# Planner costs, a merged activation block and per-block B tiles on GpSimd in a two-layer state-space kernel

## The chip, the cores and the metric

The kernel runs on one core of a Trainium2 chip. The core has a matrix engine (PE, with its weight loads shown as PEld), a vector engine (DVE), an activation engine (ACT), GpSimd (POOL) and a sync engine (SP) that issues DMAs. Each engine works through its own queue of instructions in order, and semaphores tie the queues together. The metric is the device time of one execution in microseconds, as the median of several runs.

## What is computed

Two layers on x of shape 8 x 48 x 48 x 192, all in float32. Each layer normalises its input by groups, applies a selective state-space block and adds the result to its input. The heart of both is a scan over tokens, with 384 channels and 16 states a channel. Layer 0 runs it in four directions over the image (rows, columns, both reversed):

```
xi, z = split(in_proj(x)); z = silu(z); xi = silu(conv3x3(xi))
for each of 4 directions:
    dts, B, C = x_proj(xs);  dt = softplus(dt_w @ dts + bias)
    h = exp(dt * A) * h + (dt * u) * B        # state by state, along the tokens
    y = sum over states of h * C              # + D * u
y = layernorm(y0 + y1 + y2 + y3) * z;  out = out_proj(y)
```

Layer 1 runs the same kind of scan along columns and then along rows, each forward and backward, with a causal convolution of three taps along the line:

```
xs, z = split(in_proj(x)); u = silu(conv(xs) + cb)
dt, B, C = split(x_proj(u)); dt = softplus(dt_proj(dt) + dtb)
h = h * exp(dt * A) + (dt * u) * B;  y = sum over states of h * C + u * D
y = y * silu(z);  out = out_proj(y)     # forward and backward are added
```

## The kernel before

**Tiling.** Channels lie on the 128 partitions in three groups (NJ = 3); tokens are cut into chunks of 384 (T). One chunk in one direction is an item. Each layer has 192 items. In layer 1 two items, forward and backward of the same chunk, make a pair, and there are 96 pairs: 48 for the columns and 48 for the rows. An item consists of 48 segments: 16 states by three channel groups. A due time in the code is counted in segments, so a pair spans 96.

**What a segment needs.** ACT makes the decay exp(dt * A) for one state and channel group (L423). The other factor of the scan, dt * u * B, is built with tokens on partitions, because there B of one state is one number for each partition. The product dt * u is made by POOL (du, L363), turned by PE and copied out as dtu. For each state a tile bT of three 128 x 384 blocks holds dtu times B. Either ACT makes it in three instructions with a scale for each partition (L452), or POOL makes it in one multiply of 128 x 1152 with B as a broadcast operand (L447). PE turns the blocks back into PSUM (b, L471), three transposes for a segment, and DVE runs the scan (L987 in layer 0, L1224 in layer 1). After three scans POOL multiplies all of h by C (L506), and PE adds it up over the states by transposing it into y (L523). One of the 16 states goes another way: B itself is turned, and DVE multiplies it by du (L482).

**Around the scans.** For each pair, project (L294 to L349) computes dt, B and C on PE (xd_ps, bt_ps, dt_ps), evicts them from PSUM on ACT or DVE, sends B and C to DRAM to be spread again by SP (cc), and ends with softplus on dt. In layer 1, inputs makes the convolution's input (xi_ps, L1114; taps on ACT and DVE, L1133 and L1139), gates makes z (z_ps, L1164), and begins applies silu to u of a pair and to z of the pair before it in one block on ACT (L1207) and then calls project. The function leave copies y out and turns it back; finish multiplies by z (L1228); output projects it (o_ps, L1256). Softplus and silu need another activation table than exp does: each block loads its table or tables, and then the one of exp again (L212).

**The order.** All of it is emitted by hand in an order that a planner (class Plan) makes while the program is built. Each piece of work is a Need: a due time, a cost for each engine that may take it, and the marks that it waits for. The planner keeps a clock for each engine. At each step it takes the engine that could start earliest, and gives it the ready Need with the earliest due time, within a margin NEAR. A mark counts for another engine only LAG later. So the costs in the code do two things: they choose between ACT, DVE and POOL where a Need has several, and they set in which order each engine's queue is written. COPY and BIAS are the costs of evictions, TABLE that of a table load, MM that of one pass of a wide matrix product. The function pace spreads the due times of a series of Needs over a range lo to hi.

**Depths.** Decays have 12 buffers in layer 0 and 16 in layer 1. The tiles bT have three and four; PSUM tiles b three; h four; in layer 1, u five and z four; input tiles xt three.

Of the kernel before, what the change touches and what calls it, by code (L numbers as in the profile page):

```python
# [11 lines left out]
F32 = mybir.dt.float32  # L12
# [28 lines left out]
LAG = {PE: 0.3, DVE: 0.2, ACT: 0.2, POOL: 0.2, SP: 0.0}  # L41
DMA = 3.5
NEAR = 0.2
TABLE = 1.29
COPY = {ACT: 0.41, DVE: 0.5}
BIAS = {ACT: 0.51, DVE: 0.6}
# [134 lines left out]
class Common:  # L181
# [97 lines left out]
    def project(self, plan, pool, p, pair, lo, mid, hi):  # L279

        nc, mark = self.nc, plan.mark
        tiles = {}
        dts, evacs = [], []
        for i, item in enumerate(pair):
# [34 lines left out]
            n = Need(at(), {ACT: 0.3, DVE: 0.35}, after, frees=k, sets=[mark("bt", g)])  # L321
# [5 lines left out]
            for j in range(NJ):  # L327
                after = [got]
                if j == 0 and g >= 3:
                    after.append(mark("exp", (g - 2) * NSEG - 1))  # L330
                n = Need(at(), {PE: 0.55}, after, bank=True)
                yield n
                ps = self.bank(n, "dt_ps")
                if j == 0:
                    dt = pool.tile([P, NJ, T], F32, tag="dt", name="dt", bufs=3)
                    dts.append(dt)
                nc.tensor.matmul(  # L337
                    ps[:, :T], wts["dtw"][:, j * P : (j + 1) * P], xd[:R, :], start=True, stop=True
                )
                evacs.append(plan.then(  # L340
                    Need(at(), BIAS, [n], frees=n.bank),
                    lambda e, dt=dt, j=j, ps=ps, wts=wts: self.biased(
                        e, dt[:, j, :], ps[:, :T], wts["dtb"][:, j : j + 1]
                    ),
                ))
            self.xd_used = [n, sent]
        yield Need(hi, {ACT: 2 * 1.16 + 2 * TABLE}, evacs, sets=[mark("dt", 2 * p), mark("dt", 2 * p + 1)])
        for item, dt in zip(pair, dts):
            nc.scalar.activation(dt, dt, AF.Softplus)  # L349
            item["dt"] = dt  # L350
        self.tables()
# [38 lines left out]
    def stream(self, plan, pool, items, direct, decay, scan, finish, held, kept, weighed):  # L390
# [34 lines left out]
        def weighs():  # L425
            past = []
            for i, item in enumerate(items):
                for n in states:
                    b = 0
                    while b < TB:  # L430
                        after = [mark("dtu", i, b), mark("bt", i)]
                        costs = {ACT: 0.51}
                        if b == 0:
                            if len(past) >= weighed:
                                after += [mark("place", past[-weighed] + j) for j in range(NJ)]
                            after += [mark("dtu", i, c) for c in range(1, TB)]
                            costs[POOL] = 2.2
                        need = Need(
                            i * NSEG + NJ * n - 5 + b * 0.5, costs, after, sets=[mark("bT", i, n, b)],
                            late={ACT: LATE},  # L440
                        )
                        yield need
                        if b == 0:
                            to = bts[i, n] = pool.tile([P, TB, DI], F32, tag="bT", name="bT", bufs=weighed)
                        of, by = item["dtu"], item["bt"][:, :, R + n : R + n + 1]
                        if need.e == POOL:
                            nc.gpsimd.tensor_tensor(to, of, by.to_broadcast((P, TB, DI)), ALU.mult)  # L447
                            for b in range(1, TB):
                                m = mark("bT", i, n, b)
                                m.t, m.e = need.t, need.e  # L450
                        else:
                            nc.scalar.activation(to[:, b, :], of[:, b, :], AF.Copy, scale=by[:, b, :])  # L452
                        b += 1
                    past.append(i * NSEG + NJ * n)
# [18 lines left out]
        def scans():  # L473
            for s in range(total):
# [3 lines left out]
                if n in direct:  # L478
                    done = [mark("multiplied", i)] if n == max(direct) and j == NJ - 1 else ()
                    yield Need(s, {DVE: 0.55}, [mark("place", s), mark("du", i)], sets=done)  # L480
                    b = bps[s][:, :T]
                    nc.vector.tensor_tensor(b, b, item["du"][:, j, :], ALU.mult)  # L482
# [11 lines left out]
        def gathers():  # L494

            for f in range(total // NJ):
# [3 lines left out]
                if "carry" in item:  # L500
                    yield Need(NJ * f + 2.5, {POOL: 0.19}, after, sets=[mark("carry", i, n)])
                    item["carry"](n, hs[f])
                yield Need(NJ * f + 3, {POOL: 2.64}, after + [mark("cc", i, n // 2)], sets=[mark("gather", f)])
# [75 lines left out]
def layer0(ctx, cm, x, xs, x2, w, norm):  # L579
# [43 lines left out]
    def matrices(j, due, after):  # L623

        diag = None
        for t in range(9):
            n = Need(due, {POOL: 0.4}, after)
            yield n
            if t == 0:
                diag = pool.tile([P, 9, P], F32, tag="diag", name="diag", bufs=1)  # L630
            nc.gpsimd.tensor_tensor(
                diag[:, t, :], cm.ident, cw[:, j, t : t + 1].to_broadcast((P, P)), ALU.mult
            )
# [95 lines left out]
    def convolved(diag, of, c, after, at):  # L729
        for t in range(9):  # L730
            n = Need(at(), {PE: 0.49}, after if t == 0 else (), bank=(t == 0))
# [101 lines left out]
    def enters():  # L833

        for p in range(len(items) // 2):
# [3 lines left out]
            if q < 3:  # L839
# [8 lines left out]
                yield Need(lo, {ACT: 2.13 + 2 * TABLE}, after, sets=[mark("u", b, q)])  # L848
# [3 lines left out]
            yield from cm.project(plan, pool, p, items[g : g + 2], lo, mid, hi)  # L852

    def tails():
# [4 lines left out]
        for b in range(NIMG):  # L859
            st = None  # L860
            for c in range(NC - 1, -1, -1):
# [13 lines left out]
                n = Need(at(), {DVE: 1.45}, [n], frees=k)  # L875
# [4 lines left out]
                n = Need(at(), {ACT: 1.16}, [n] + used)  # L880
# [16 lines left out]
                n = Need(at(), {DVE: 1.77}, [n])  # L897
# [13 lines left out]
                n = Need(at(), {ACT: 1.16 + 2 * TABLE}, [got_z])  # L911
# [4 lines left out]
                for j in range(NJ):  # L916
                    n = Need(at(), {POOL: 1.0}, [n])
# [47 lines left out]
    for b in range(NIMG):  # L965
        for k in range(4):
            rev = k >= 2
            order = range(NC - 1, -1, -1) if rev else range(NC)
            for n, c in enumerate(order):
# [5 lines left out]
                    cost=(0.75, 3.1, 0.96) if k % 2 else (0.65, 2.64, 0.96),  # L975
# [16 lines left out]
    def finish(i, item, j, need, y):  # L992
        b, k, c = item["b"], item["k"], item["c"]

        def add(e):
# [9 lines left out]
            Need(need.due + 1, {DVE: 0.85 if k % 2 else 0.6}, [need], frees=need.bank,  # L1005
# [12 lines left out]
def layer1(ctx, cm, x2, xw, dst, w, norm):  # L1018
# [53 lines left out]
    def inputs():  # L1072

        last = []
        for p in range(pairs):
            stage, b, c = place_of(p)
            lo, hi = 2 * p * NSEG - 176, 2 * p * NSEG - 96
# [15 lines left out]
            if stage == 0:  # L1093
                n = Need(at(), {ACT: 1.02}, [n])
# [32 lines left out]
    def taps(i, j, u, ps, k, n, at):  # L1127
# [3 lines left out]
        n = Need(plan.at + 1, {ACT: 0.51}, [n])  # L1131
# [4 lines left out]
        n = Need(plan.at + 1, {DVE: 2 * 0.59}, [n], frees=k, sets=[mark("tapped", i, j)])  # L1136
# [7 lines left out]
    def gates():  # L1144

        last = []
        for p in range(pairs):
            stage = place_of(p)[0]
            lo, hi = 2 * p * NSEG - 76, 2 * p * NSEG + 2
# [5 lines left out]
            for d in range(2):  # L1155
                for j in range(NJ):
                    for m in range(NM):
                        after = [mark("x", p), wz[d][1]] + ([mark("out", p - 2)] if p > 1 else [])
# [9 lines left out]
                    if j == 0:  # L1168
                        z = items[2 * p + d]["z"] = pool.tile([P, NJ, T], F32, tag="z", name="z", bufs=4)
# [6 lines left out]
    def begins():  # L1176

        last, block = [], [mark("never")]
        diag = None
        for p in range(pairs + 1):  # L1180
            stage = place_of(p)[0]
            s = 2 * p * NSEG
            if p % per == 0 and p < pairs:
                xp, n0 = yield from part("xp", w["xp"][:, 2 * stage : 2 * stage + 2], s - 100, cm.xd_used)
                dtw, n1 = yield from part("dtw", w["dtw"][:, 2 * stage : 2 * stage + 2], s - 100, cm.xd_used)
                n = Need(s - 90, {DVE: 1.5})
# [5 lines left out]
            after = []  # L1192
            for d in range(2):
                if p < pairs:
                    after += [mark("tapped", 2 * p + d, j) for j in range(NJ)]
                if p > 0:
                    after += [mark("gate", 2 * p - 2 + d, j) for j in range(NJ)]
            if 0 < p < pairs:
                after.append(mark("exp", s - 96 + 18))
            count = 2 * (p > 0) + 2 * (p < pairs)  # L1200
            done = [mark("silu", 2 * p - 2)] if p > 0 else ()
            n = Need(s - 87, {ACT: 2 * TABLE + 1.16 * count}, after, sets=done)
            yield n
            for d in range(2):
                for i, name in ((2 * p + d, "own"), (2 * p - 2 + d, "z")):
                    if 0 <= i < len(items) and (name == "z") == (i < 2 * p):
                        nc.scalar.activation(items[i][name], items[i][name], AF.Silu)  # L1207
            cm.tables()
            if p == pairs:
                return  # L1210
            for d in range(2):
                items[2 * p + d].update(
                    diag=diag[:, d], A=A[:, 2 * stage + d], ready=[n] + loaded,
                    wts=dict(xp=xp[:, d], dtw=dtw[:, d], dtb=dtb[:, 2 * stage + d]),
                )
            yield from cm.project(plan, pool, p, items[2 * p : 2 * p + 2], s - 84, s - 52, s - 30)
# [9 lines left out]
    def finish(i, item, j, need, y):  # L1226
# [3 lines left out]
        plan.then(Need(need.due + 1, {DVE: 0.55}, [need], frees=need.bank, sets=[mark("gated", i, j)]), gate)  # L1230
# [3 lines left out]
    def output(p):  # L1234
# [13 lines left out]
        for m in range(NM):  # L1248
# [12 lines left out]
            n = Need(at(), {DVE: 0.6}, [n] + (got if stage else before), frees=k)  # L1261
# [14 lines left out]
        dict(cost=(0.65, 2.64, 0.9), wanted=lambda j, i=i: [mark("silu", i - i % 2)]) for i in range(2 * pairs)  # L1276
# [81 lines left out]
```

## Time and profile before

| | us |
|---|---|
| median of 3 runs | 21915.49 (21907.13 to 21929.59) |
| profiled execution, its own time | 21913.88 |
| span in the profile | 21912.2 |
| first scan of layer 1 | 11120 after the start |

The costliest groups of instructions, with the mean duration of one:

| engine and line | what | count | busy us | mean ns |
|---|---|---|---|---|
| POOL L506 | h times C, 128 x 1152 | 6144 | 16183.7 | 2647 |
| DVE L1224 | scan, layer 1 | 9216 | 8149.8 | 936 |
| PE L471 | B tiles turned into PSUM | 51840 | 8090.6 | 277 |
| ACT L452 | B tile, one block | 13998 | 8067.2 | 608 |
| PE L523 | sum over states | 55296 | 7944.2 | 276 |
| ACT L423 | decays, both layers | 18432 | 10338.2 | 602 to 608 |
| POOL L363 | du | 384 | 1075.2 | 2800 |
| ACT | table loads, all lines | 755 | 968.7 | 1283 |

Durations overlap: the next instruction of an engine often starts before the one before it has ended. On ACT, six decays in a row take 3.09 us together, so they start 0.50 us apart, while each lasts 0.60. A busy engine is therefore not necessarily one at its limit, and distances between starts say more about what it can do than durations do. DMA moves 69 GB/s on average, with the 16 engines at about a fifth of their time. The TensorE clock granted is 0.992.

### The profile page before, as it was taken

How to read it: one execution, taken by the hardware profiler on the slowest of the kernel's cores; microseconds unless marked ns; L12 is line 12 of the kernel's file. 1: busy time of each engine (PE TensorE's matmuls, PEld its weight loads, DVE VectorE, ACT ScalarE, POOL GpSimd, SP SyncE). 2: the span in 40 equal slices, each digit the busy share in tenths (PEclk: the TensorE clock that was granted, in tenths of full speed). 3: DMA queues.
4: the chain of work that ended last, by engine and by line, in shares of the span. 5: the costliest groups of instructions: out<-in, count | busy, mean ns of one | idle time of the engine just before them, and what ended most of it. 6: DMA issues, size and time to landing. Idle time of an engine off the chain costs nothing.

```text
span 21912.2 us, 391042 instructions
## 1 busy us (share of the span) xinstructions
PE 20543.4 (94%) x138640; PEld 15779.7 (72%) x138640; DVE 19575.8 (89%) x24030; ACT 20649.0 (94%) x38918; POOL 20082.0 (92%) x10562
## 2 busy tenths in 40 slices
PE   9989899899998999988889999999999999999999
PEld 6767667676676766766667777777777777777777
DVE  7998898989889898899978888888888999999998
ACT  7999999999999999999989999999999999999999
POOL 7999999999999999999979999999999999999999
PEclk9999999999999999999999999999999999999999
DMA  2222222222222222221222221211122222222222
GB/s 76 75 83 68 75 78 74 83 68 74 77 74 83 68 75 76 74 74 61 66 61 63 62 63 62 63 62 62 62 64 65 66 66 66 66 65 66 66 66 64
DMA packets 728901, 1512.31 MB, mean 69 GB/s; under 512 B 181508, under 2 KB 324484, under 8 KB 726824
## 3 DMA queue, kind: packets, MB, share of 16 engines
q1 hardware_dynamic: 724768, 1485.21, 21.7%
q8 instruction: 1105, 18.10, 0.3%
q14 instruction: 844, 6.91, 0.1%
q10 hardware_dynamic: 2184, 2.08, 0.0%
HBM read 1382.03 MB, written 104.99 MB: 68 GB/s over the span
## 4 chain that ended last, share of the span: by engine, by line
PE 55%; ACT 21%; POOL 11%; DVE 7%; issue 5%; DMA 1%; POOLq 0%; DVEq 0%; SPq 0%; ACTq 0%
PE y L523 16%; PE b L471 16%; POOL h L506 9%; ACT bT L452 8%; ACT l_da L423 5%; PE xd_ps L294 4%; ACT a L423 4%; PE dt_ps L337 4%; PE cv_ps L735 4%; DVE h L1224 3%; PE o_ps L1256 3%; PE z_ps L1164 2%; DVE h L987 2%; PE xi_ps L1114 2%; PE xi_ps L684 1%
## 5 line engine op out<-in xcount | busy, mean ns | idle before, releaser
L506 POOL TENSOR_TENSOR h<-h,cc 128x1152 f32<-128x1152 f32 x6144 | 16183.7, 2647 | 988.3 <-DVE h L1224 346.8
L1224 DVE TENSOR_TENSOR_SCAN h<-l_da,b 128x384 f32<-128x384 f32 x9216 | 8149.8, 936 | 709.6 <-PE b L471 541.8
L471 PE MATMUL b<-ident,bT 128*128 128x128 f32 x51840 | 8090.6, 277 | 471.2 <-DVE h L987 311.9
L523 PE MATMUL y<-ident,h 128*128 128x128 f32 x55296 | 7944.2, 276 | 621.2 <-POOL h L506 588.2
L452 ACT ACTIVATE bT<-dtu,bt 128x384 f32<-128x384 f32 x13998 | 8067.2, 608 | 77.9 <-PE b L471 67.9
L523 PEld LDWEIGHTS y<-ident,h 128*128 128x128 f32 x55296 | 6310.9, 141 | 2189.2 <-POOL h L506 1176.6
L471 PEld LDWEIGHTS b<-ident,bT 128*128 128x128 f32 x51840 | 6061.7, 141 | 2411.4 <-issue 971.6
L987 DVE TENSOR_TENSOR_SCAN h<-a,carry,b 128x384 f32<-128x384 f32 x7680 | 7223.1, 995 | 636.3 <-PE b L471 299.0
L423 ACT ACTIVATE a<-dt,l_A 128x384 f32<-128x384 f32 x9216 | 5220.6, 608 | 27.5 <-DVE h L987 25.4
L423 ACT ACTIVATE l_da<-dt,l_A 128x376 f32<-128x376 f32 x9216 | 5117.6, 602 | 77.6 <-DVE h L1224 75.5
L447 POOL TENSOR_TENSOR bT<-dtu,bt 128x1152 f32<-128x1152 f32 x1094 | 2324.2, 2125 | 200.8 <-PE b L471 174.9
L987 DVE TENSOR_TENSOR_SCAN h<-a,b 128x384 f32<-128x384 f32 x1536 | 1359.9, 936 | 166.5 <-PE b L471 114.4
L294 PE MATMUL xd_ps<-u,l_xp 128*44 128x384 f32 x2304 | 1128.8, 586 | 3.9 <-ACT u L1133 2.7
L363 POOL TENSOR_TENSOR du<-dt,u 128x1152 f32<-128x1152 f32 x384 | 1075.2, 2800 | 62.3 <-ACT dt L349 61.6
L337 PE MATMUL dt_ps<-xd,l_dtw 12*128 12x384 f32 x2304 | 1043.5, 534 | 10.4 <-ACT z L220 8.0
L1114 PE MATMUL xi_ps<-xt,l_u 96*128 96x384 f32 x2304 | 936.3, 490 | 12.7 <-ACT xt L1097 6.3
L735 PE MATMUL cv_ps<-pad,diag 128*128 128x384 f32 x2376 | 939.2, 490 | 0.5 <-ACT v L227 0.3
L1256 PE MATMUL o_ps<-z,l_out 128*96 128x384 f32 x2304 | 931.7, 489 | 0.9 <-ACT dt L227 0.8
L962 POOL COPY carry<-h 128x3 f32<-128x3 f32 x2560 | 504.4, 197 | 442.1 <-DVE h L987 303.4
L1164 PE MATMUL z_ps<-xt,l_z 96*128 96x384 f32 x2304 | 885.3, 489 | 1.1 <-ACT xd L220 0.6
L227 ACT ACTIVATE dt<-dt_ps,l_dtb 128x384 f32<-128x384 f32 x931 | 539.8, 580 | 292.5 <-PE dt_ps L337 283.8
L1139 DVE SCALAR_TENSOR_TENSOR u<-xi_ps,l_conv_w,u 128x376 f32<-128x376 f32 (+1 forms) x1152 | 686.6, 596 | 65.4 <-ACT u L1133 43.4
(122 smaller groups left out, 14499.2 us busy)
## 6 DMA issues: line engine op xcount, KB each, us to landing
cc<-bc SPq DMA_DIRECT2D x3072, 384.0 KB, 3.5
xc<-in_x SPq DMA_DIRECT2D x186, 288.0 KB, 4.4
z<-v SPq DMA_DIRECT2D x144, 192.0 KB, 1.9
z<-z SPq DMA_DIRECT2D x48, 576.0 KB, 4.3
v<-v SPq DMA_DIRECT2D x126, 192.0 KB, 1.8
u<-v SPq DMA_DIRECT2D x21, 1152.0 KB, 8.3
xc<-in_xs SPq DMA_DIRECT2D x48, 288.0 KB, 3.6
x<-xc SPq DMA_DIRECT2D x48, 288.0 KB, 3.0
```

Of the source, the lines that this page charges most:

```text
L294: nc.tensor.matmul(rows(ps[:E, :T]), wts["xp"][:, j, :], item["u"](j), start=(j == 0), stop=(j == NJ - 1),)
L337: nc.tensor.matmul(ps[:, :T], wts["dtw"][:, j * P : (j + 1) * P], xd[:R, :], start=True, stop=True)
L423: nc.scalar.activation(dst, src, AF.Exp, scale=item["A"][:, j, n : n + 1])
L447: nc.gpsimd.tensor_tensor(to, of, by.to_broadcast((P, TB, DI)), ALU.mult)
L452: nc.scalar.activation(to[:, b, :], of[:, b, :], AF.Copy, scale=by[:, b, :])
L471: nc.tensor.transpose(ps[:, b * P : (b + 1) * P], of, self.ident)
L506: nc.gpsimd.tensor_tensor(h, h, c, ALU.mult)
L523: nc.tensor.matmul(item["sum"][b][:, j * P : (j + 1) * P], hs[f][:, j, b * P : (b + 1) * P], self.ident, is_transpose=True, skip_group_che ...
L735: nc.tensor.matmul(rows(ps[:, :T]), diag[:, t, :], of[:, c * RT + t // 3 : (c + 1) * RT + t // 3, t % 3 : t % 3 + S], start=(t == 0), stop ...
L987: nc.vector.tensor_tensor_scan(order(h[:, at % NJ, :]), order(a), order(b[:, :T]), carry[:, at : at + 1] if item["carried"] else 0.0, ALU. ...
L1224: nc.vector.tensor_tensor_scan(h[:, at % NJ, :], a, b[:, :T], 0.0, ALU.mult, ALU.add)
L1256: nc.tensor.matmul(ps[:CP, :T], wout[:, 2 * stage + e, j, m * CP : (m + 1) * CP], items[2 * p + e]["z"][:, j, :], start=(e == 0 and j == 0 ...
```

## The change

Four things change.

1. The numbers that the planner reckons with are replaced nearly everywhere: lags, the margin, costs of copies, bias evictions, scans, projections and so on.
2. In weighs, each 128 x 384 block of bT is now a Need of its own that ACT or POOL may take. POOL does one block by a tensor_scalar instruction whose scalar is a column of B, in place of one tensor_tensor over the whole tile.
3. project no longer ends with softplus. In layer 0, enters does it at the same place. In layer 1 a new function block puts softplus of a pair, silu of that pair's z and silu of the next pair's u behind one another on ACT, with a table load for softplus, one for silu and one back to exp at the end. Only the first pair's are still done in parts.
4. In layer 1, the due times of inputs, gates and project lie earlier; z has six buffers in place of four, and a pair's z waits for the output of three pairs before in place of two.

```diff
-LAG = {PE: 0.3, DVE: 0.2, ACT: 0.2, POOL: 0.2, SP: 0.0}
+LAG = {PE: 0.2, DVE: 0.14, ACT: 0.15, POOL: 0.1, SP: 0.0}
-NEAR = 0.2
+NEAR = 0.1
-COPY = {ACT: 0.41, DVE: 0.5}
-BIAS = {ACT: 0.51, DVE: 0.6}
+COPY = {ACT: 0.37, DVE: 0.47}
+BIAS = {ACT: 0.48, DVE: 0.53}
...
-                n = Need(at(), {PE: 0.55}, after, bank=True)
+                n = Need(at(), {PE: 0.83}, after, bank=True)
...
-        yield Need(hi, {ACT: 2 * 1.16 + 2 * TABLE}, evacs, sets=[mark("dt", 2 * p), mark("dt", 2 * p + 1)])
         for item, dt in zip(pair, dts):
-            nc.scalar.activation(dt, dt, AF.Softplus)
             item["dt"] = dt
-        self.tables()
+        return evacs
...
-                        costs = {ACT: 0.51}
-                        if b == 0:
-                            if len(past) >= weighed:
-                                after += [mark("place", past[-weighed] + j) for j in range(NJ)]
-                            after += [mark("dtu", i, c) for c in range(1, TB)]
-                            costs[POOL] = 2.2
+                        if b == 0 and len(past) >= weighed:
+                            after += [mark("place", past[-weighed] + j) for j in range(NJ)]
                         need = Need(
-                            i * NSEG + NJ * n - 5 + b * 0.5, costs, after, sets=[mark("bT", i, n, b)],
-                            late={ACT: LATE},
+                            i * NSEG + NJ * n - 5 + b * 0.5, {ACT: 0.51, POOL: 0.6}, after,
+                            sets=[mark("bT", i, n, b)], late={ACT: LATE},
                         )
...
-                            nc.gpsimd.tensor_tensor(to, of, by.to_broadcast((P, TB, DI)), ALU.mult)
+                            nc.gpsimd.tensor_scalar(to[:, b, :], of, by, None, ALU.mult)
...
-                    cost=(0.75, 3.1, 0.96) if k % 2 else (0.65, 2.64, 0.96),
+                    cost=(1.29, 3.1, 0.915) if k % 2 else (0.7, 2.6, 0.915),
...
-            lo, hi = 2 * p * NSEG - 176, 2 * p * NSEG - 96
+            lo, hi = 2 * p * NSEG - 230, 2 * p * NSEG - 146
...
-            lo, hi = 2 * p * NSEG - 76, 2 * p * NSEG + 2
+            lo, hi = 2 * p * NSEG - 130, 2 * p * NSEG - 50
...
-            yield from cm.project(plan, pool, p, items[2 * p : 2 * p + 2], s - 84, s - 52, s - 30)
+            after = yield from cm.project(plan, pool, p, items[2 * p : 2 * p + 2], s - 120, s - 80, s - 46)
+            if p == 0:
+                yield from block(s - 44, here, [], [], after)
+                yield from block(s - 10, [], here, there)
+            else:
+                yield from block(s - 44, here, here, there, after + [mark("exp", s - 36)])
+
+    def block(due, dts, zs, us, after=()):
+
+        after = list(after) + [mark("gate", i, j) for i in zs for j in range(NJ)]
+        after += [mark("tapped", i, j) for i in us for j in range(NJ)]
+        sets = [mark("dt", i) for i in dts] + [mark("silu z", i) for i in zs] + [mark("silu", i) for i in us]
+        tables = 1 + bool(dts) + bool(zs or us)
+        yield Need(due, {ACT: tables * TABLE + 1.07 * len(dts + zs + us)}, after, sets=sets)
+        cm.softplus([items[i] for i in dts])
+        for i in zs:
+            nc.scalar.activation(items[i]["z"], items[i]["z"], AF.Silu)
+        for i in us:
+            nc.scalar.activation(items[i]["own"], items[i]["own"], AF.Silu)
+        cm.tables()
...
-        dict(cost=(0.65, 2.64, 0.9), wanted=lambda j, i=i: [mark("silu", i - i % 2)]) for i in range(2 * pairs)
+        dict(cost=(0.71, 2.6, 0.855), wanted=lambda j, i=i: [mark("silu z", i)]) for i in range(2 * pairs)
```

## The prediction

> **What bounds the kernel now.** I read the page's first part, then busy time in stretches, then the timeline of one stretch. The first part names no single bound:
>
> ```profile
> PE 20543.4 (94%) x138640; PEld 15779.7 (72%) x138640; DVE 19575.8 (89%) x24030; ACT 20649.0 (94%) x38918; POOL 20082.0 (92%) x10562
> ```
>
> Four engines are nearly full, so what matters is whether they are full at the same moments. Layer 0 ends with its last scan at 11007 us; layer 1 begins scanning at 11120 and repeats every 112.2 us, once per pair of items (96 pairs). One such pair, cut in four, columns being the stretch, its length, then busy time and instructions by engine:
>
> ```profile
> 14962.00:14990.00 28.00, 26.52 (x193) 20.95 (x192) 23.46 (x30) 27.94 (x49) 27.85 (x12) 1.00 0.20 59
> 14990.00:15018.00 28.00, 28.00 (x177) 20.76 (x177) 25.65 (x36) 24.61 (x49) 24.65 (x10) 1.00 0.24 70
> 15018.00:15046.00 28.00, 28.00 (x186) 20.91 (x185) 24.66 (x31) 25.58 (x49) 23.39 (x10) 1.00 0.24 65
> 15046.00:15075.00 29.00, 27.86 (x212) 23.85 (x211) 27.84 (x38) 28.80 (x56) 28.39 (x12) 1.00 0.17 56
> ```
>
> In the middle half PE (first column) never rests, and ACT and POOL (fourth and fifth) lose 3.4 + 2.4 and 3.4 + 4.6 us. In the outer half ACT and POOL are full and PE is not. The bound alternates. The timeline of ACT, DVE and POOL shows what the middle looks like:
>
> ```profile
> 15018.53 1.63 ACT L452 ACTIVATE bT<-dtu,bt 128x384 f32<-128x384 f32 x3 [1.72 <-PE b L471]
> 15024.30 0.95 DVE L1224 TENSOR_TENSOR_SCAN h<-l_da,b 128x384 f32<-128x384 f32 x1 [1.15 <-PE b L471]
> 15019.79 2.63 POOL L506 TENSOR_TENSOR h<-h,cc 128x1152 f32<-128x1152 f32 x1 [3.33 <-issue]
> ```
>
> Everyone waits for PE's transposes (L471), which stand in PE's queue behind projections (o_ps, dt_ps, xi_ps, z_ps, xd_ps all fall there); POOL's row names no releaser, but what it multiplies are the scans that come late. At the start of each pair it is ACT that holds things up, with a block of silus between two table loads; a scan waits for the exponential behind it:
>
> ```profile
> 15089.31 1.28 ACT L1207 ACT_TABLE_LOAD   x1
> 15090.60 1.17 ACT L1207 ACTIVATE u<-u 128x1152 f32<-128x1152 f32 x1
> ...
> 15094.95 1.28 ACT L212 ACT_TABLE_LOAD   x1
> 15096.24 5.11 ACT L423 ACTIVATE l_da<-dt,l_A 128x376 f32<-128x376 f32 x10
> 15096.88 1.80 DVE L1224 TENSOR_TENSOR_SCAN h<-l_da,b 128x384 f32<-128x384 f32 x2 [0.92 <-ACT l_da L423]
> ```
>
> **What each engine must do.** For every form I take its step, the lower quartile of the time from its start to the next start on its engine; this leaves waits out. Steps times counts over 60 steady pairs give, per pair of 112.2 us: ACT 105.1, PE 103.4, POOL 102.7, DVE 99.4. (PE: 612 transposes by 0.109, 36 diagonal products by 0.111, 72 wide passes by 0.322, 12 of dt_ps by 0.412, 12 of xd_ps by 0.357, 6 small.) The rest is loss: ACT 7.1, PE 8.8, POOL 9.5, DVE 12.8. In layer 0, over 300 to 11000 us, the same sums are POOL 93.6%, ACT 93.0%, DVE 88%, PE 81%.
>
> **The change, part by part.** Counts are from the two programs' instruction orders.
>
> Merged block, layer 1: table loads fall from 382 to 285, so ACT saves 97 x 1.295 = 126 us. The activations in it are the same.
>
> New planner costs: in layer 1 ACT hands DVE 105 bias evictions, 80 xd, 113 yt, 65 z and 84 small copies. ACT saves 50 + 30 + 41 + 23 + 13 us (steps 0.479, 0.376, 0.36, 0.36, 0.15). DVE pays about 56 + 38 + 51 + 30 + 14 us, with some dtu copies 199: 2.1 us a pair. In layer 0 it is 124 bias evictions and 32 of v, ACT about -68, DVE about +82 us, which its 12% of slack there hides.
>
> B tiles: ACT makes 242 blocks less in layer 0 and 97 less in layer 1 (0.506 each: -122 and -49 us). POOL goes from 419 whole tiles to 1501 blocks, and from 675 to 2120. Its old tile has a step of 2.058 us in layer 0 and 2.072 in layer 1. The new operation is nowhere in the trace, so I bound it. Rows on POOL:
>
> ```profile
> L447 POOL TENSOR_TENSOR bT<-dtu,bt 128x1152 f32<-128x1152 f32 x1094 | 2324.2, 2125 | 200.8 <-PE b L471 174.9
> L631 POOL TENSOR_TENSOR diag<-ident,l_conv_w 128x128 f32<-128x128 f32 x207 | 79.8, 417 | 90.8 <-PE cv_ps L735 90.8
> L919 POOL TENSOR_TENSOR acc<-acc,z 128x384 f32<-128x384 f32 x144 | 142.6, 1005 | 22.5 <-ACT z L913 22.5
> L777 POOL MEMSET acc<- 128x5000 f32 x1 | 4.3, 4264 | 0.0
> ```
>
> Upper end: a multiply with a broadcast operand has steps 0.358 at 128 elements and 2.072 at 1152, hence 1.674 ns an element and 0.144 us fixed; at 384, 0.787 us. Lower end: the two memsets (2181 ns at 2500, 4264 at 5000) give 0.83 ns and 0.10 us, at 384 0.42 us. In between: two full streams cost 2.14 ns an element (steps 0.954 at 384, 2.60 at 1152), a step-zero second one 1.67; dropping it saves as much again, 1.20 ns, so 0.46 + 0.144 = 0.60 us. I take 0.60, since the broadcast multiply, from which this is drawn down, is the nearest kin. POOL then changes by 901 - 862 = +39 us in layer 0 and 1272 - 1399 = -127 in layer 1.
>
> The Trainium skill (GPSIMD Engine Reference, 4.1 Engine selection) calls one-input work on this engine roughly line-rate; at the 1.2 GHz of its Specifications that is, as an estimate, 0.32 us plus dispatch for 384 elements, and with the trace's 0.10 us fixed POOL would fall by some 230 us in layer 0 and 510 in layer 1. Against the change speaks its section 2.1 Instruction dispatch, by which every instruction pays a software call of tens of cycles: three blocks pay it three times. The trace's own fixed part, 0.144 us, already holds that. No row here shows the operation itself.
>
> Moved work: input projections are due 54 to 50 segments earlier, z projections 54 or 52, dt and B projections up to 36. Pair-relative (96 segments) the input projections leave 16 to 96 for 58 to 142, the z ones 20 to 98 for 62 to 142, the others 12 to 66 for 72 to 146. So PE's extras leave the crowded middle for the stretch where PE now loses 5.6 of its 8.8 us. Loads of xt move on SP past nine cc loads; SP carries 64 GB/s and no row has a scan waiting for it, so I price that at nothing.
>
> The block itself: 6 x 1.07 + 3 x 1.295 = 10.3 us in which ACT makes no exponential and no B block. Behind it stand the exponentials that the scans need, and DVE waits for those. Its cover is 16 decay buffers and four B tiles, twelve segments, or 14 us at 1.17 us a scan, and POOL goes on making B blocks. It lands near segment 52, where ACT today has slack; the old 6.9 us one lies where ACT has none. If the cover is empty, it costs up to 10.3 us a pair, less the 2.7 us that DVE loses around the old one.
>
> **The sum.** Layer 1 per pair: ACT 105.1 - 341/96 = 101.5 (the 341 also holds 25 dtu copies, 9 us), POOL 102.7 - 1.3 = 101.4, DVE 101.5, PE still 103.4, now the longest. What is lost on top: in the 22 of 32 slices where PE now sets the pace it loses 3.2 us, which over a whole pair is 4.6; ACT, today's longest, loses 7.1. I take 5.9 between them: 109.3 us, 2.9 less, x 96 = -280 us. Layer 0: if POOL alone sets the end, +39/0.936 = +42 us; if POOL and ACT share the B work freely, (39 - 190)/2/0.93 = -81; midway, -20. Together -300 against the profiled span of 21912.2 us: 21612. Its run took 21913.9 and the median of the three shown is 21915.5, so I say 21,615. Own range, ends 108.0 and 110.5 us a pair, layer 0 -81 to +42: 21,430 to 21,795.
>
> By the Trainium skill (Perfetto Trace Analysis, Identifying the Most-Contended Engine) matmul busy time is no measure of headroom and weight-load time is. The four stretches have 86.5 us of weight loads in 113, so by it PE would not be the longest, and 101.5 + 5.9 would give 107.4 us and -460 for layer 1. The waits above, on PE's results, contradict it.
>
> **Rivals.** (1) Slower: a POOL block costs like the broadcast multiply, 0.787 us. The planner reckons 0.6, so it does not take blocks back. Layer 0: 1181 - 862 = +319, /0.936 = +341. Layer 1: POOL 102.7 + 2.8 = 105.5, + 5.9 = 111.4, -0.8 x 96 = -80. Sum +261: 22,175. It decides from 0.72 us, where the two cancel. For it: nearest kin in the trace. Against: one stream less. Chance 0.20.
> (2) No gain: PE keeps its loss of 8.8 us, as DVE with 2.1 us more work in order makes PE wait for PSUM: 112.2 again, only layer 0's -20: 21,895. For it: four engines within 2 us of each other leave no slack. Chance 0.13.
> (3) More: spreading removes most loss, 106.5 us a pair and layer 0 at -81: -630, 21,285. For it: DVE's and POOL's losses are mostly waits for PE in the crowded middle. Chance 0.12.
> (4) The merge does not happen: the order shows the three loads and six activations in a row. Nothing.
> My forecast: 0.55.
>
> **Range and chances.** 0.2% is 44 us, about what a measurement here can tell from none. Faster: 0.55 + 0.12 and half of (2) and a little of (1), 0.74; same 0.08; slower 0.18. The range goes to near rival (3) and to (2): 21,340 to 21,900.
>
> **What will show it.** ACT table loads 660; POOL's B blocks at a 0.60 us step (0.72 and more proves me wrong); pairs of layer 1 at about 109 us; no long ACT, POOL or DVE waits for L471's transposes in mid-pair; DVE not waiting for exponentials after the block. A layer 0 over 11,050 us, or a pair still at 112, breaks the sum.

## The result, and the profile after

The changed kernel takes 23,181 us (median of 4 runs, 23,160 to 23,183) against 21,918 before: a ratio of 1.057, with a 95% interval of 1.056 to 1.059. It is slower by 1,263 us, where the prediction had 21,615 and a range that ended at 21,900. The page's first part, and its rows of the two operations that now make up POOL's work:

```profile
PE 21033.9 (91%) x138640; PEld 16046.1 (69%) x138640; DVE 19938.8 (86%) x24644; ACT 20291.3 (88%) x37870; POOL 22185.4 (96%) x13089
L500 POOL TENSOR_TENSOR h<-h,cc 128x1152 f32<-128x1152 f32 x6144 | 16159.7, 2640 | 631.8 <-DVE h L1225 230.6
L445 POOL TENSOR_SCALAR bT<-dtu,bt 128x384 f32<-128x384 f32 x3621 | 4497.1, 1251 | 73.4 <-PE b L465 52.9
```

The first row no longer shows four engines side by side: POOL is at 96%, and ACT has fallen from 94 to 88%. The last row says why. A block takes POOL 1251 ns, and 1.21 us from its start to the next start; for this step the prediction had 0.60 us and 0.787 at the most. The 3,621 blocks come to 4,497 us, against 2,324 us for the 1,094 whole tiles before.

One steady pair of layer 1, cut in four as in the prediction (stretch, length, then PE, PEld, DVE, ACT, POOL):

```profile
15121.00:15151.00 30.00, 28.98 (x203) 22.41 (x202) 25.66 (x34) 27.44 (x56) 29.81 (x15) 1.00 0.18 56
15151.00:15181.00 30.00, 29.14 (x182) 21.39 (x181) 24.62 (x34) 25.52 (x50) 23.49 (x13) 1.00 0.23 63
15181.00:15211.00 30.00, 27.23 (x178) 20.95 (x176) 24.78 (x35) 25.43 (x40) 30.00 (x16) 0.94 0.15 50
15211.00:15242.00 31.00, 28.01 (x196) 22.10 (x194) 28.70 (x38) 28.40 (x56) 31.00 (x15) 1.00 0.21 63
```

POOL has no idle moment in the last two stretches, and everyone else has. PE no longer fills the middle half. The granted TensorE clock is 0.977 over the whole run, 0.992 before; 1.5% of the 103.4 us that PE's steps need of a pair would be 1.6 us, and PE now loses 17, so this is not what makes the pair longer. The timeline of POOL in the last stretch shows what it is full of:

```profile
15225.30 2.52 POOL L445 TENSOR_SCALAR bT<-dtu,bt 128x384 f32<-128x384 f32 x2
15227.74 2.68 POOL L500 TENSOR_TENSOR h<-h,cc 128x1152 f32<-128x1152 f32 x1
15230.33 1.30 POOL L445 TENSOR_SCALAR bT<-dtu,bt 128x384 f32<-128x384 f32 x1
15231.54 10.49 POOL L500 TENSOR_TENSOR h<-h,cc 128x1152 f32<-128x1152 f32 x4
```

Two blocks put one after the other step by 1.22 us (2.44 us from the first row's start to the second's), and a tile of three would be 3.6 us where the old multiply took 2.07. Downstream, the sum over states waits for POOL. From the list of waits, first before, then after (longest in total, times, longest):

```profile
PE y L523 <- POOL h L506: 588.2, 1133, 2.5
```

```profile
PE y L517 <- POOL h L500: 1460.3, 1885, 4.0
```

By the same steps as in the prediction, POOL now needs 115.2 us of a pair of 120.5 and loses 5.2. The others lose 17 to 19. The first scan of layer 1 starts at 11,628 us instead of 11,121.

### The profile page after: what moved, and what is told of

It is laid out like the page before. It is cut to its first block, busy times and chain, and to the rows that moved or that the text cites. A ratio compares the mean times of both kernels' runs of the same rounds, so it can differ in the third digit from the quotient of the medians.

```text
span 23177.6 us, 394817 instructions
## 1 busy us (share of the span) xinstructions
PE 21033.9 (91%) x138640; PEld 16046.1 (69%) x138640; DVE 19938.8 (86%) x24644; ACT 20291.3 (88%) x37870; POOL 22185.4 (96%) x13089
## 5 line engine op out<-in xcount | busy, mean ns | idle before, releaser
L517 PE MATMUL y<-ident,h 128*128 128x128 f32 x55296 | 8310.3, 281 | 1511.0 <-POOL h L500 1460.3
L1225 DVE TENSOR_TENSOR_SCAN h<-l_da,b 128x384 f32<-128x384 f32 x9216 | 8267.3, 938 | 1097.5 <-PE b L465 943.6
L517 PEld LDWEIGHTS y<-ident,h 128*128 128x128 f32 x55296 | 6394.2, 143 | 3559.7 <-POOL h L500 2949.0
L465 PE MATMUL b<-ident,bT 128*128 128x128 f32 x51840 | 8306.1, 280 | 408.1 <-DVE h L985 193.1
L447 ACT ACTIVATE bT<-dtu,bt 128x384 f32<-128x384 f32 x13659 | 7854.2, 606 | 370.6 <-PE b L465 318.9
L465 PEld LDWEIGHTS b<-ident,bT 128*128 128x128 f32 x51840 | 6212.1, 144 | 2041.8 <-issue 737.6
L445 POOL TENSOR_SCALAR bT<-dtu,bt 128x384 f32<-128x384 f32 x3621 | 4497.1, 1251 | 73.4 <-PE b L465 52.9
L1112 PE MATMUL xi_ps<-xt,l_u 96*128 96x384 f32 x2304 | 847.6, 494 | 34.5 <-DVE u L1137 24.3
L476 DVE TENSOR_TENSOR b<-b,du 128x384 f32<-128x384 f32 x1152 | 629.7, 547 | 195.9 <-PE b L465 190.6
L1131 ACT ACTIVATE u<-xi_ps,l_conv_b,l_conv_w 128x384 f32<-128x384 f32 x576 | 385.0, 669 | 392.0 <-PE xi_ps L1112 390.1
```

The lines of the kernel that those rows point to most:

```text
L445: nc.gpsimd.tensor_scalar(to[:, b, :], of, by, None, ALU.mult)
L447: nc.scalar.activation(to[:, b, :], of, AF.Copy, scale=by)
L465: nc.tensor.transpose(ps[:, b * P : (b + 1) * P], of, self.ident)
L517: nc.tensor.matmul(item["sum"][b][:, j * P : (j + 1) * P], hs[f][:, j, b * P : (b + 1) * P], self.ident, is_transpose=True, skip_group_che ...
L1225: nc.vector.tensor_tensor_scan(h[:, at % NJ, :], a, b[:, :T], 0.0, ALU.mult, ALU.add)
```

## The experiments

The times in this table are medians of four runs. The ratios are to runs of the kernel before that were made beside them, with medians of 21,913 to 21,918 us. "Layer 1 starts" is its first scan, "pair" the mean over 60 steady pairs, and the last column counts the B tiles or blocks that POOL made.

| kernel | us | ratio to before (95%) | layer 1 starts | pair | on POOL |
|---|---|---|---|---|---|
| before | 21,915 | 1 | 11,121 | 112.2 | 1,094 tiles |
| changed | 23,181 | 1.056 to 1.059 | 11,628 | 120.5 | 3,621 blocks |
| e_whole | 21,356 | 0.973 to 0.976 | 10,894 | 109.3 | 1,070 tiles |
| e_cost | 21,684 | 0.988 to 0.991 | 11,028 | 110.9 | 2,403 blocks |
| e_scalar_only | 23,334 | 1.063 to 1.066 | 11,602 | 121.9 | 3,786 blocks |
| e_merge | 21,702 | 0.989 to 0.992 | 11,103 | 110.4 | 1,006 tiles |
| e_costs | 21,536 | 0.981 to 0.984 | 10,861 | 111.0 | 1,186 tiles |
| e_block_tt | 21,519 | 0.980 to 0.983 | 10,875 | 110.6 | 3,164 blocks |
| e_misprice | 22,183 | 1.010 to 1.013 | 11,173 | 114.9 | 1,336 tiles |
| e_oldpe | 22,028 | 1.004 to 1.007 | 11,202 | 112.6 | 1,186 tiles |
| e_oldlag | 21,654 | 0.987 to 0.990 | 10,883 | 112.3 | 1,124 tiles |
| e_carry | 21,337 | 0.972 to 0.975 | 10,865 | 109.3 | 995 tiles |

**The operation alone.** A kernel of its own, of which this is the core, shortened: each line stands for 24 instructions in a row on `size` elements of each partition.

```
for size in (128, 384, 1152):
    tensor_scalar(ptr, a, s[:, 20:21], None, mult)
    tensor_scalar(imm, a, 2.0, None, mult)
    tensor_tensor(bcast, a, s[:, 20:21].to_broadcast((P, size)), mult)
    tensor_tensor(full, a, c, mult)
    tensor_copy(copied, a)
```

> GpSimd alone, no other engine at work: five forms at 128, 384 and 1152 elements a partition, 24 of each in a row. The scans are left out, and zeros are written as the output. Theory A (the new operation itself is slow): tensor_scalar with a scalar from SBUF steps about 1.2 us at 384 also here, the broadcast multiply 0.69 to 0.79, two streams 0.95. Theory B (it is slow only beside the scans, by contention with DVE): tensor_scalar steps 0.6 us or less at 384. The form with a number written in the instruction tells whether the fetch of the scalar (then it is cheap) or the operation itself (then it costs the same) is what is slow; the sizes tell a fixed price from one per element.

From the groups by line and form (count, busy us, mean ns):

```profile
L34 POOL TENSOR_SCALAR ptr<-a,s 128x1152 f32<-128x1152 f32 x24 | 76.6, 3193 | 0.0
L36 POOL TENSOR_SCALAR imm<-a 128x1152 f32<-128x1152 f32 x24 | 74.9, 3119 | 0.0
L42 POOL TENSOR_TENSOR full<-a,c 128x1152 f32<-128x1152 f32 x24 | 62.5, 2605 | 0.0
L38 POOL TENSOR_TENSOR bcast<-a,s 128x1152 f32<-128x1152 f32 x24 | 50.4, 2102 | 0.0
L34 POOL TENSOR_SCALAR ptr<-a,s 128x384 f32<-128x384 f32 x24 | 29.7, 1239 | 0.0
L36 POOL TENSOR_SCALAR imm<-a 128x384 f32<-128x384 f32 x24 | 27.9, 1164 | 0.0
L44 POOL COPY copied<-a 128x1152 f32<-128x1152 f32 x24 | 27.5, 1147 | 1.4
L42 POOL TENSOR_TENSOR full<-a,c 128x384 f32<-128x384 f32 x24 | 23.7, 988 | 0.0
L38 POOL TENSOR_TENSOR bcast<-a,s 128x384 f32<-128x384 f32 x24 | 19.7, 822 | 0.0
L44 POOL COPY copied<-a 128x384 f32<-128x384 f32 x24 | 12.0, 499 | 0.0
```

Theory A holds. The block is as slow with no other engine at work (1239 ns, step 1189) as in the kernel (1251). It is not the fetch of the scalar: a number written in the instruction saves 75 ns. It is a price per element: 2.54 ns from 384 to 1152 elements ((3193 - 1239) / 768), against 1.67 for the broadcast multiply, 2.1 for two streams and 0.84 for a copy, all by durations. Why this operation is dearer, no run shows. The broadcast multiply's measured 0.793 us step at 384 is the 0.787 that the prediction worked out.

**The change without its B tiles (e_whole).**

```diff
-                            i * NSEG + NJ * n - 5 + b * 0.5, {ACT: 0.51, POOL: 0.6}, after,
+                        costs = {ACT: 0.51}
+                        if b == 0:
...
+                            costs[POOL] = 2.07
...
-                            nc.gpsimd.tensor_scalar(to[:, b, :], of, by, None, ALU.mult)
+                            nc.gpsimd.tensor_tensor(to, of, by.to_broadcast((P, TB, DI)), ALU.mult)
```

> The changed kernel with the B tiles as before: POOL makes a whole tile by one broadcast multiply (planned at 2.07 us), all other parts of the change kept. Theory A (the per-block tensor_scalar at 1.21 us is the whole loss, the rest is the gain that was forecast): 21,450 to 21,800 us, layer 1 near 109 us a pair. Theory B (the merged block or the new costs lose as well): over 21,900 us, layer 1 at 112 us a pair or more.

21,356 us: below theory A's range, and 558 us below before. Layer 1 runs at 109.28 us a pair, layer 0 is 227 us shorter. POOL's row of B tiles, one pair in four parts, and the merged block on ACT, with what DVE does after it:

```profile
L450 POOL TENSOR_TENSOR bT<-dtu,bt 128x1152 f32<-128x1152 f32 x1070 | 2264.5, 2120 | 60.8 <-PE b L474 41.8 <-DVE dtu L222 13.3 <-PE y L526 1.6
```

```profile
15125.00:15152.00 27.00, 27.00 (x197) 21.78 (x197) 24.30 (x31) 26.35 (x53) 25.67 (x12) 1.00 0.23 63
15152.00:15179.00 27.00, 27.00 (x169) 19.80 (x167) 25.00 (x34) 26.25 (x53) 22.76 (x11) 1.00 0.20 56
15179.00:15206.00 27.00, 26.71 (x198) 21.55 (x196) 25.84 (x34) 26.59 (x42) 26.41 (x11) 1.00 0.26 76
15206.00:15234.00 28.00, 26.37 (x186) 21.34 (x185) 27.15 (x37) 26.93 (x56) 26.54 (x11) 1.00 0.21 65
```

```profile
15182.65 1.28 ACT L354 ACT_TABLE_LOAD   x1
15183.95 2.22 ACT L354 ACTIVATE dt<-dt 128x1152 f32<-128x1152 f32 x2
...
15191.81 1.28 ACT L212 ACT_TABLE_LOAD   x1
15193.11 3.61 ACT L426 ACTIVATE l_da<-dt,l_A 128x376 f32<-128x376 f32 x7
```

```profile
15192.82 5.42 DVE L1234 TENSOR_TENSOR_SCAN h<-l_da,b 128x384 f32<-128x384 f32 x6
15199.03 1.80 DVE L1234 TENSOR_TENSOR_SCAN h<-l_da,b 128x384 f32<-128x384 f32 x2 [0.79 <-ACT l_da L426]
```

PE (the first column) is now near full in all four parts, not only in the middle, and ACT has work in all four. The block lasts from 15182.65 to 15193.1, 10.4 us. DVE works on through all of it and pays one wait of 0.79 us some five us after its end: the cover of decays and B tiles held, almost to the last one. Over all of layer 1 it held as well. DVE's scans waited 9.2 us in total for decays, and 40.4 in the kernel before:

```profile
L1234 DVE TENSOR_TENSOR_SCAN h<-l_da,b 128x384 f32<-128x384 f32 x9216 | 8162.5, 936 | 441.0 <-PE b L474 337.3 <-POOL h L509 13.6 <-ACT l_da L426 9.2
```

```profile
L1224 DVE TENSOR_TENSOR_SCAN h<-l_da,b 128x384 f32<-128x384 f32 x9216 | 8149.8, 936 | 709.6 <-PE b L471 541.8 <-ACT l_da L423 40.4 <-POOL bT L447 21.7
```

**The change with the true price (e_cost).**

```diff
-                            i * NSEG + NJ * n - 5 + b * 0.5, {ACT: 0.51, POOL: 0.6}, after,
+                            i * NSEG + NJ * n - 5 + b * 0.5, {ACT: 0.51, POOL: 1.21}, after,
```

> The changed kernel with the planner told 1.21 us for a POOL block in place of 0.6, nothing else. Theory A (POOL is overfilled because the planner does not know the price): POOL gets about half the blocks, ACT the others, and the time falls to 21,700 to 22,200 us, since a block at 1.21 is still dearer than 0.69 in a whole tile. Theory B (something else holds it): it stays above 22,700 us.

21,684 us, just below theory A's range.

```profile
L445 POOL TENSOR_SCALAR bT<-dtu,bt 128x384 f32<-128x384 f32 x2403 | 2986.3, 1247 | 76.0 <-PE b L465 46.7 <-DVE dtu L222 14.9 <-DVE dt L229 9.1
```

The operation is as slow as in the changed kernel (1247 ns), but POOL gets 2,403 blocks instead of 3,621 (two thirds, not half) and needs 106.3 us a pair instead of 115.2. So of the 1,825 us between the changed kernel and e_whole, one number in the planner is worth 1,497, and the operation's own price and its form of one block at a time, once priced, 328.

**The B tiles alone, on the kernel before (e_scalar_only).** The function weighs is that of the change, all else that of before.

> The kernel before with only the B tiles of the change: one block each, POOL by tensor_scalar, planned at 0.6 us. Theory A: this part alone loses all of it and more, since the savings on ACT are missing: 23,100 to 23,700 us. Theory B (the order of the merged block and the costs is the main loss): under 22,500 us.

23,334 us, as theory A had it. This part alone costs 1,420 us. Added to it, the rest of the change brings 153 us, while without it the rest brings 558: where POOL sets the pace, time saved on ACT and waits taken off PE are mostly worth nothing.

**The wrong price with the right operation (e_misprice).** As e_whole, but:

```diff
-    costs[POOL] = 2.07
+    costs[POOL] = 1.03
```

> The changed kernel with whole B tiles by the broadcast multiply, which takes 2.07 us, but the planner told 1.03, half of it, as the change does with its block (0.6 for 1.21). Theory A (the loss is the planner's wrong price, not the operation): POOL gets over 1,500 tiles in place of about 1,090 and the time rises to 22,400 to 23,300 us. Theory B (the dear operation itself is the loss): within 1% of the run with the right price, 21,150 to 21,570 us.

22,183 us, between the ranges of the two theories. The direction is theory A's: 826 us lost to a number that changes no instruction's duration (a tile takes 2118 ns, in e_whole 2120). The size is not: POOL made 1,336 tiles, not over 1,500.

```profile
L450 POOL TENSOR_TENSOR bT<-dtu,bt 128x1152 f32<-128x1152 f32 x1336 | 2822.3, 2118 | 89.5 <-PE b L474 60.4 <-ACT dtu L220 11.7 <-DVE dtu L222 11.0
```

By steps, POOL needs 104.8 us of a pair of 114.9 here and loses 10.1, so over a pair it is not overfilled. In single stretches it is. Two stretches of one steady pair, and what POOL does in the second:

```profile
18193.00:18202.50 9.50, 9.50 (x56) 6.85 (x55) 8.53 (x12) 7.36 (x14) 5.44 (x3) 1.00 0.27 72
18231.00:18240.50 9.50, 6.52 (x45) 4.63 (x44) 7.48 (x11) 8.09 (x14) 9.50 (x5) 1.00 0.11 41
```

```profile
18230.80 6.25 POOL L450 TENSOR_TENSOR bT<-dtu,bt 128x1152 f32<-128x1152 f32 x3
```

POOL is idle for almost half of the first stretch. In the second it makes three tiles one after the other, which the planner put at 3.1 us and which take 6.25; POOL is full and PE is down to 6.5 of 9.5 us. So a wrong price harms although the engine has time to spare over a pair: it puts too much work into one stretch. How much of the 826 us comes this way, and how much from the rest of the order, no run separates.

**One block at a time by the broadcast multiply (e_block_tt).**

```diff
-                            i * NSEG + NJ * n - 5 + b * 0.5, {ACT: 0.51, POOL: 0.6}, after,
+                            i * NSEG + NJ * n - 5 + b * 0.5, {ACT: 0.51, POOL: 0.79}, after,
...
-                            nc.gpsimd.tensor_scalar(to[:, b, :], of, by, None, ALU.mult)
+                            nc.gpsimd.tensor_tensor(to[:, b, :], of, by.to_broadcast((P, DI)), ALU.mult)
```

> The changed kernel with B tiles one block at a time, but POOL does a block by the broadcast multiply, planned at 0.79 us (measured alone: 0.793 for a block, 2.063 for a tile, 0.688 a block). Theory A (price alone counts): somewhat dearer than the whole tile, 21,380 to 21,520 us. Theory B (a finer grain gives a better fit): under 21,330 us.

21,519 us, at the upper end of theory A. Measured alone, a block costs 0.79 us, or 0.69 as part of a tile, and the finer grain doesn't make up for it: e_whole is 162 us faster.

**What the gain of e_whole consists of (e_merge, e_costs).** e_merge has the kernel before with the new block, due times and z buffers, but the old costs, except that it counts an activation of softplus or silu at 1.07 us where the kernel before has 1.16. e_costs is its complement: only the other numbers.

> The kernel before with the merged block, the earlier due times and the six z buffers of layer 1, but its own planner costs and whole B tiles. Layer 0 is then as before. Theory A (layer 1's gain comes from where the block and PE's projections lie): layer 1 at 109 to 110.5 us a pair, first scan of layer 1 at 11,120 us as before, 21,630 to 21,760 us in all. Theory B (the measured costs bring it): layer 1 stays at 111.5 us or more, over 21,840 us.

> The kernel before with the new planner costs alone: whole B tiles (planned at 2.07 us), separate softplus and silu blocks, old due times. Theory A (costs bring layer 0's gain, the block layer 1's): first scan of layer 1 at about 10,890 us, layer 1 at 111 to 112.5 us a pair, 21,600 to 21,720 us. Theory B (costs also bring layer 1's): layer 1 under 110.3 us a pair, under 21,520 us.

e_merge takes 21,702 us and 110.4 us a pair, as theory A had it. e_costs takes 21,536 us: layer 0 as expected, 111.0 us a pair at the lower end, and the sum 64 us below the range. A pair gains 1.8 us by the one and 1.2 by the other, and 2.9 by both. In total -211 and -377 make -588 where both together give -558. Nearly all of layer 0's gain is in the numbers: its length falls by 18 us in e_merge and by 260 in e_costs.

**Which numbers (e_oldpe, e_oldlag).** Each is e_costs with some of the old numbers. In e_oldpe these are PE's costs of dt_ps, of the convolution of layer 0 (cv_ps) and of xd_ps (the first number of each `cost`, in layer 0 and in layer 1):

```diff
-                n = Need(at(), {PE: 0.83}, after, bank=True)
+                n = Need(at(), {PE: 0.55}, after, bank=True)
...
-            n = Need(at(), {PE: 0.65}, after if t == 0 else (), bank=(t == 0))
+            n = Need(at(), {PE: 0.49}, after if t == 0 else (), bank=(t == 0))
...
-                    cost=(1.29, 3.1, 0.915) if k % 2 else (0.7, 2.6, 0.915),
+                    cost=(0.75, 3.1, 0.915) if k % 2 else (0.65, 2.6, 0.915),
...
-        dict(cost=(0.71, 2.6, 0.855), wanted=lambda j, i=i: [mark("silu", i - i % 2)]) for i in range(2 * pairs)
+        dict(cost=(0.65, 2.6, 0.855), wanted=lambda j, i=i: [mark("silu", i - i % 2)]) for i in range(2 * pairs)
```

In e_oldlag they are the lags and the margin:

```diff
-LAG = {PE: 0.2, DVE: 0.14, ACT: 0.15, POOL: 0.1, SP: 0.0}
+LAG = {PE: 0.3, DVE: 0.2, ACT: 0.2, POOL: 0.2, SP: 0.0}
...
-NEAR = 0.1
+NEAR = 0.2
```

> The run with the new planner costs alone (21,536 us), with PE's four projection costs back at the old values (xd_ps 0.65 and 0.75, dt_ps 0.55, cv_ps 0.49). Theory A (layer 0 gained 256 us because the planner now knows what PE's projections take, above all xd_ps in the odd directions, 1.29 for 0.75): the first scan of layer 1 goes back to 11,030 us or later, total over 21,680 us. Theory B (lags and margin, or the costs of ACT and DVE, brought it): first scan of layer 1 under 10,930 us, total under 21,600 us.

> The run with the new planner costs alone (21,536 us), with the old lags (0.3, 0.2, 0.2, 0.2) and margin (0.2). Theory A (PE's costs brought layer 0's gain): within 60 us of it, 21,480 to 21,600 us. Theory B (lags and margin brought it): first scan of layer 1 back at 11,030 us or later, total over 21,680 us.

With PE's old costs layer 1 starts at 11,202 us, 341 later than in e_costs and even later than before: the other new numbers without these lose. So PE's costs carry layer 0; which of the four does it was not tried. With the old lags layer 0 stays (10,883), but layer 1 falls back to 112.3 us a pair, so the total misses theory A's range by 54 us. With PE's old costs layer 1 falls back too, to 112.6: its share of the numbers' gain needs both, the lags and PE's costs.

**One more wrong number (e_carry).** POOL's copies of the carry step by 0.27 us and are planned at 0.15. e_carry is e_whole with their measured value.

> The changed kernel with whole B tiles (21,356 us), with the cost of POOL's carry copy at 0.27 us, its measured step, in place of 0.15. Theory A (the planner's unpriced POOL time costs some 0.6 us for each us, as the mispriced tiles did): 2,560 copies by 0.12 are 307 us, so layer 0 gains 100 to 200 us, 21,150 to 21,260 us. Theory B (layer 0 is held by something else): within 50 us of 21,356.

21,337 us against 21,356, with intervals that overlap: theory B, and no 0.6 us for each us unpriced. Why this wrong number is nearly harmless and the other isn't was not tried. It is the lowest median of all.

## Why the prediction was wrong

**The step that failed** is the price of the new operation: "at 384, 0.787 us" as the upper end, "0.42 us" as the lower, and "I take 0.60". It is 1.19 to 1.22. Both ends rested on the idea that what an operation costs on POOL follows from the streams it reads, and so that one stream less must be cheaper than the broadcast multiply. The trace of before had no tensor_scalar on POOL at all, and the upper end was a different instruction that computes the same; nothing in those rows excluded that the instruction itself is slower. A bound from rows of another operation bounds only what the two have in common.

**The rest of layer 1's sum stood, in part by luck.** With 1.21 put in, the prediction's formula gives POOL 102.7 - 14.6 + 22.1 x 1.21 = 114.8, with 5.9 of loss 120.7 us a pair; measured 120.5. With POOL out of the way it said PE 103.4 with 5.9 of loss, 109.3; e_whole has PE 103.4, lost 5.9, 109.28. The steps held. That the loss fits so closely is luck: 5.9 was taken between 4.6 and 7.1, and the engine with the longest steps loses 4.6 us in e_cost (POOL), 5.5 in e_merge (ACT), 8.3 in e_oldpe (ACT) and 10.1 in e_misprice (POOL). Nor does the sum show that PE alone sets the pace in e_whole: ACT, which makes 14,070 blocks there and not the 13,659 of the changed kernel, needs 103.2 us a pair.

Of the sources that it named, the block's place and PE's spread bring 1.8 us a pair (e_merge). The planner's costs bring 1.2 (e_costs), but not by relieving ACT alone, as the prediction had it: in e_oldpe the new costs of evictions stay and ACT needs 104.3 us, as against 104.1 in e_costs, and yet the pair is at 112.6 again.

**Layer 0 was sized wrong both ways.** By the formula with 1.21, (1816 - 862) / 0.936 = +1,019 us; measured +507. The share of POOL need not stay at 93.6%: in the changed kernel its steps fill 97.3% of 300 to 10,900 us, and at that share the formula comes to some +570 ((0.936 x 10,700 + 954) / 0.973 - 10,700). In the other direction, without the slow blocks layer 0 gains 227 us (e_whole), and e_oldpe ties this to PE's costs in the planner (with the old ones layer 1 starts at 11,202 us). The prediction had -81 as its best case: it costed the evictions that changed engine, and gave a better order no value in layer 0. While POOL is full the gain does not appear: layer 1 starts at 11,628 us in the changed kernel and at 11,602 in e_scalar_only.

**Rival 1** had the mechanism and its condition: POOL at a price the planner does not know, deciding from 0.72 us. Its price was bounded at 0.787, so it ended at 22,175 instead of 23,181. Its remark that the planner "does not take blocks back" is what e_cost shows: told the price, it takes 1,218 back and the time falls by 1,497 us.

**Rivals 2 and 3** did not come. In e_whole PE loses 5.9 us, not the 8.8 of rival 2, and DVE, which takes on the evictions, some 9 where it lost 12.8. Rival 3 had layer 1 at 106.5 us a pair. Its total, 21,285 us, is near e_whole's 21,356 all the same, because layer 0 gains 227 us there and not 81.

**The block's cover** was costed at nothing, with 10.3 us if it is gone: in e_whole's pair above it costs 0.79 us of DVE's time, where the old block's wait after the table load was 0.92, and over all of layer 1 the waits for decays fall from 40.4 to 9.2 us.

**Its signs.** The table loads came to 660 as it said (95 fewer in layer 1, where it counted 97). POOL's step of 1.21 us and layer 0's 11,628 us are two of those by which it said that it would be wrong.

**On the Trainium skill's rules:** GPSIMD Engine Reference, 4.1 Engine selection, has one-input work at roughly line-rate; the copy agrees (0.84 ns an element), the tensor_scalar does not (2.54), and the measurement decides. Perfetto Trace Analysis, Identifying the Most-Contended Engine, has MFU (matmul work done over the peak) and weight-load time rather than matmul time as the measure of PE; by weight-load time the prediction had layer 1 at 107.4 us a pair without PE as its limit. e_whole has 109.28. Weight loads are at 84.5 of 109 us in the pair shown, PE's steps at 103.4: PE has less headroom than the weight loads alone would say.

## What to carry to other kernels

Before an operation that the trace doesn't show is given to an engine, measure it alone, with a few sizes and its nearest relatives: a kernel of half a millisecond (457 us) tells what no row of the old profile could. Where a planner writes the order of in-order queues from a table of durations, a wrong number there is a performance bug like any other: it was worth 1,497 us here while the operation stayed the same, and 826 us with the cheaper operation. A part that fills one engine hides what the other parts gain (153 us instead of 558), so parts of a change are to be timed one by one.

## What was not expected of the hardware

On GpSimd a tensor_scalar multiply costs 2.54 ns an element, more than a tensor_tensor multiply of two full streams (2.1) and half as much again as one with a broadcast operand (1.67), though it reads less. With the scalar written into the instruction it is 2.55. A copy costs 0.84 by durations and 0.97 by steps. The fixed part of the tensor_scalar, 0.20 us by its steps (1.189 - 384 x 2.57), is no more than a fifth of what a block costs. What makes the rest of it so dear is open.
